# Two pairs of heads one behind the other, with unloads behind the first mask operation and sums over keys in the shares of products

## Chip, core and metric

The kernel runs on one core of one Trainium2 chip. The metric is the device time of one execution in microseconds (us); lower is better. A core has engines that each work through a queue of their own in order and wait for each other by semaphores: TensorE (PE in the profile, its weight loads PEld), VectorE (DVE), ScalarE (ACT), GpSimd (POOL) and SyncE (SP, which issues the transfers here). The products write to PSUM[...].

## The reference

The input x holds 32 batches of 512 rows by 512 features; adj is a 512 x 512 matrix of zeros and ones. Two layers are computed, in float32.

```python
q, k, v = x @ Wq + bq, x @ Wk + bk, x @ Wv + bv          # 8 heads of 64
scores  = einsum(q, k) / 8 + where(adj == 0, -1e9, 0)
x = layernorm(x + einsum(softmax(scores), v))            # layer 0
norm_adj = adj * rsqrt(deg)[:, None] * rsqrt(deg)[None, :]
x = layernorm(x + norm_adj @ (x @ weight) + bias)        # layer 1
```

## The kernel before

All work is one stream over **blocks**. A block is a batch b and a pair of heads g; the eight heads make four pairs, taken in ORDER = (0, 2, 1, 3), so that 32 batches give S = 128 blocks, and `at = k % 4` is the place of block k within its batch. The loop over k writes the program of all engines out by hand: the four compute engines are wrapped in `InOrder`, which pins each instruction to the place where the code issues it. Transfers on SP are not pinned.

**What one turn of the loop does.** `scores(k)` makes the scores of a block in two halves (jj = 0, 1) of two tiles each: per tile TensorE multiplies keys with queries for two heads at once (64 rows each), VectorE takes the minimum with 60 and subtracts the mask (255 where adj is zero), and ScalarE takes the exponential in place. Between the two halves stands `fold` of the block before: VectorE transposes the sums over keys in 32 x 32 blocks and reduces them. Then `values(k - 1)` multiplies the exponentials of the block before with the values (64 columns for each head); the products of a block add up in one PSUM bank, the tile "av" (one buffer). VectorE then unloads that bank by a transpose into "yb" (one buffer), and four transfers on SP put yb into the rows of YT. `accumulate` lets GpSimd add the exponentials over the four tiles of a block; half of that is put off (`pending`, `put_off`) to places in the work that follows, and what is still pending is drained at the top of the next turn.

**The share.** Behind the attention products of each turn, `run(shares.pop(0))` runs a share of all other work: values, keys and queries of the next batch (`values_of`, `keys_and_queries`, each seven pieces of products with a half-size scheme of sums and differences), the normalising of the batch before (`finish`: inverse, scale, add, measure, root, norm, low, lift, judge), and its graph product (`convolve`: first, parts, second, measure, root, store). A list `side` is written out by hand once a batch, at `at == 1`: the pieces of `main` in order, with `beside` giving by number what follows a piece. `cut` splits it by counting pieces with products: eight to a share, four shares to a batch. A piece takes the next PSUM buffer by turns of three buffers of two banks ("wide") and one of one bank ("narrow"); the score tiles take the same three wide buffers.

**Buffers that matter here.** "e" holds exponentials, six buffers, so three halves of blocks; a half's buffers come free when its `values` products and its `accumulate` are done. "acc" has two buffers, freed by `fold`. "kq" has five, "yT" two.

**Lines.** Every instruction passes through the wrapper at line 44, so the profile's lines tell nothing and its rows are told apart by tile names: "sc" are score tiles, "av" the values' sums, "mm" the other products, "e<-sc,maskT" the mask operation, "acc" the sums over keys, "folded" their reduction, "yb<-av" the unload, "parts" sums and differences ahead of the graph product's second half, "lo" and "hi" the two parts of its first factor.

Of the kernel before, what the change touches and what calls it, by code (L numbers as in the profile page):

```python
# [49 lines left out]
def unshifted(  # L50
# [29 lines left out]
    B, N, D = x.shape  # L80
    NT = N // P
    DT = D // P
    G = H // 2
# [315 lines left out]

    E, ACC, AV, SM, YT, HI, LO = {}, {}, {}, {}, {}, {}, {}  # L400

    def scores(s):

        b, g, jj = s
        E[s] = [work.tile([P, 2, N], F32, name="e", bufs=6) for _ in range(2)]
        for l in range(2):
            j = 2 * jj + l
            e = E[s][l]
            p = psum.tile([P, 2, N], F32, name="sc", **WIDE)
            for k in range(2):  # L410
                r = slice(k * HD, (k + 1) * HD)
                tensor.matmul(p[:, k, :], KQ[b, g][r, 0, ts(j, P)], KQ[b, g][r, 1, :], start=True, stop=True)
            vector.scalar_tensor_tensor(
                e, p, CUT, maskT[:, j, None, :].to_broadcast([P, 2, N]), op0=ALU.min, op1=ALU.subtract
            )
            scalar.activation(e, e, AF.Exp)

    def accumulate(s, ls=(0, 1)):

# [14 lines left out]
            for l in ls:  # L434
                gpsimd.tensor_add(ACC[b, g][0], ACC[b, g][0], E[s][l])

    def values(s):

        b, g, jj = s
        e = E.pop(s)  # L440
        if jj == 0:
            AV[b, g] = psum.tile([P, N], F32, name="av")
        av = AV[b, g]
        for l in range(2):
            j = 2 * jj + l
            for k in range(2):
                tensor.matmul(
                    av[k * HD : (k + 1) * HD, :], V[b][:, j, ts(2 * g + k, HD)], e[l][:, k, :],
                    start=j == 0, stop=j == NT - 1,
                )  # L450
        if jj == 0:
            return
        if (b, g) == blocks[-1]:
            turned = work.tile([P, N], F32, name="avT", tag="yb", bufs=1)
            scalar.copy(turned[:, :HALF], av[:, :HALF])
            vector.tensor_copy(turned[:, HALF:], av[:, HALF:])
            AV[b, g] = turned
            return

        yb = work.tile([P, 4, NT, 32], F32, name="yb", bufs=1)
        vector.transpose(
            yb.rearrange("p l i s -> p i l s"), av.rearrange("p (i r l) -> p i l r", i=NT, l=4)
        )
        if g == ORDER[0]:
            if b < B - 1:
                YT[b] = acts.tile([P, NT, D], F32, name="yT")
            else:
                YT[b] = wv[:, :NT].rearrange("p k u o -> p k (u o)")  # L470
        for q in range(4):
            nc.sync.dma_start(
                YT[b][:, :, (4 * g + q) * 32 : (4 * g + q + 1) * 32],
                yb[32 * q : 32 * (q + 1)],
            )
# [326 lines left out]
    def run(pieces):  # L802
        for _, f, args in pieces:
            f(*args)

    def cut(pieces, counts):

        lists = [[]]
        left = list(counts)
        for piece in pieces:  # L810
            if piece[0] > 1:
                if not left[0]:
                    left.pop(0)
                    lists.append([])
                left[0] -= 1
            lists[-1].append(piece)
        return lists
# [6 lines left out]
            accumulate(*pending.pop(0))  # L824

    put_off = [(0, more, ())]

    ORDER = (0, 2, 1, 3)
    blocks = [(b, g) for b in range(B) for g in ORDER]
# [23 lines left out]
    for k in range(S + 1):  # L853
        b, at = divmod(k, G)
        if at == 1:
            if 1 < b < B - 1:
                load_residual(b - 1)
            if b + 2 < B:
                load_x(b + 2, 0)
            if b + 1 < B:  # L860
                main, kq = keys_and_queries(b + 1, 0), keys_and_queries(b + 1, 1)
                if b:
                    main = values_of(b + 1) + main
                turn0, turn1 = turns(b + 2) if b + 2 < B else ([], [])
                main += kq[:5]
            if b == 0:
                w1_parts = [(0, weigh_part, (w1, gpsimd, i)) for i in range(4)]
                exact = [(0, compare, (m,)) for m in range(NT)]
                main += kq[5:]
                beside = {  # L870
                    0: exact[:1], 2: put_off, 3: put_off + exact[1:2], 6: put_off + [(0, degrees, ())],
                    7: w1_parts[:1] + put_off, 8: w1_parts[1:2], 9: w1_parts[2:3], 10: put_off + turn0,
                    11: put_off + w1_parts[3:], 12: exact[2:3],
                }
                inner, rest = turn1, exact[3:]
                side = early[5:6] + put_off + early[6:] + put_off
                side += sum(([piece] + beside.get(i, []) for i, piece in enumerate(main)), [])
                shares = cut(side, (4, 4, 4, 4))
            elif b < B - 1:
                f, c = finish(b - 1), convolve(b - 1)  # L880
                norm, low, grow, measure = f["norm"], f["low"], f["grow"], f["measure"]


                beside = {
                    0: rest[:1] + put_off, 1: put_off + rest[1:3], 2: rest[3:4], 3: rest[4:5] + f["inverse"],
                    4: rest[5:6] + f["scale"][:2], 5: rest[6:7] + f["scale"][2:] + f["add"], 6: rest[7:],
                    8: measure[:2] + put_off, 9: measure[2:] + f["root"] + put_off, 10: norm[:1], 11: norm[1:2],
                    12: norm[2:3] + low[:1], 13: low[1:2], 14: norm[3:] + low[2:3], 16: low[3:] + put_off,
                    17: put_off, 18: f["lift"] + turn0 + f["judge"],
                }  # L890
                side = sum(([piece] + beside.get(i, []) for i, piece in enumerate(main)), [])
                side += c["first"] + c["parts"] + grow + kq[5:] + turn1[:1]
                s = c["second"]
                if b < B - 2:
                    side += put_off + s[:1] + put_off + s[1:3] + turn1[1:2] + s[3:4] + turn1[2:3] + s[4:5]
                    side += turn1[3:4] + s[5:6] + c["measure"][:1] + turn1[4:] + s[6:]
                    rest = c["measure"][1:] + c["root"] + c["store"]
                    shares = cut(side, (8, 8, 8, 8))
                else:
                    held, h, last = c, s, finish(b)  # L900
                    scale, add = last["scale"], last["add"]
                    side += h[:1] + last["inverse"] + h[1:2] + scale[:2] + h[2:3] + scale[2:] + add
                    shares = cut(side, (8, 8, 8, 4))
            else:
                f, c, last = last, convolve(b - 1), finish(b)
                s, first, low, lift, pairs = c["second"], c["first"], f["low"], f["lift"], last["pairs"]
                within = low[:1]
                shares = [
                    h[3:4] + f["measure"] + f["root"] + h[6:] + f["norm"],
                    h[4:5] + low[1:3] + h[5:6] + low[3:] + lift + f["judge"] + put_off + put_off + last["early"] + first[:2]  # L910
                    + held["measure"][:2] + first[2:3] + held["measure"][2:] + first[3:] + c["parts"] + f["grow"],
                    held["root"] + s[:2] + pairs[0] + pairs[1],
                    [],
                ]


        while pending:
            more()
        if k == S - 2:
            load_residual(B - 1)  # L920
        if k < S:
            scores((*blocks[k], 0))
        else:
            turn_of["n"], turn_of["order"] = 0, (WIDE, dict(tag="narrow"), dict(tag="av"))
        if k == 0:
            run(two)
            early = values_of(1)
            run(early[:2])
        elif at == 1 and b:
            run(inner)  # L930
            inner = []
        if k and blocks[k - 1][0] < B - 1:
            fold(*blocks[k - 1])
        if k < S - 3:
            scores((*blocks[k], 1))
            turn_of["n"] = 0
        if k:
            values((*blocks[k - 1], 0))
            if k == S:
                sums(B - 1, 1)  # L940
            values((*blocks[k - 1], 1))
            if k == S - 2:
                sums(blocks[k - 1][0], (k - 1) % G // 2)
                run(within)
# [13 lines left out]
            load_residual(B - 2)  # L958
        if k == 0:
            run(early[2:4] + put_off + put_off + early[4:5])  # L960
        elif shares:
            run(shares.pop(0))

    count = small.tile([P, 1], F32, name="count")
# [306 lines left out]
```

## Time and profile before

| | |
|---|---|
| median of 3 runs | 2784.55 us (2784.54 to 2784.9) |
| profiled execution, its own time | 2784.45 us |
| its span in the profile | 2782.6 us, 34,623 instructions |
| busy: PE, PEld | 2760.6 us (99%), 1878.3 us (68%) |
| busy: DVE, ACT, POOL | 2232.0 us (80%), 1050.6 us (38%), 1795.6 us (65%) |
| granted TensorE clock | 0.999 |
| moved by transfers | 141.06 MB, 51 GB/s on the mean |

Busy time is the union of an engine's instructions over the span. The ends of matmuls are modelled and overlap the starts of the next, so a busy PE says that it never ran dry, not that each step is as short as it can be: steps are read from the starts. Each float32 product stands in the trace as two records, so a block shows 16 records "sc" and 16 "av" for its 8 and 8 products. The profiled execution lies within 0.1 us of the median and 1.85 us above its own span.

### The profile page before, as it was taken

To read this page: it belongs to the slowest core of one execution; us is meant where nothing else is said; L and a number is where in the kernel's file an instruction comes from. 1 tells how busy PE (TensorE), PEld (TensorE's weight loads), DVE (VectorE), ACT (ScalarE), POOL (GpSimd) and SP (SyncE) were. 2 spreads that over 40 slices of the span, in tenths; PEclk is the share of its full clock that TensorE was granted. 3 is DMA by queue.
4 is the path that set the end of the run, shared out by engine and by line. 5 is a ranking of instruction groups with operands and counts; after the bars stand their busy time and mean duration, and the time that the engine had idled before them with its cause. 6 is when DMAs were issued, how large, how long until landed. Compare 5 with 4: busy or idle time off the path is not lost.

```text
span 2782.6 us, 34623 instructions
## 1 busy us (share of the span) xinstructions
PE 2760.6 (99%) x12540; PEld 1878.3 (68%) x12540; DVE 2232.0 (80%) x3199; ACT 1050.6 (38%) x1324; POOL 1795.6 (65%) x1171
## 2 busy tenths in 40 slices
PE   9999999999999999999999999999999999999997
PEld 7666666666666666666666666666666666666665
DVE  5878877788777888777887778877788877788787
ACT  2234333343333433334433334333343433443344
POOL 3666676666666666766667666666666676666756
PEclk9999999999999999999999999999999999999999
DMA  4111122112221111211112211222111121111211
GB/s 122 35 31 45 52 59 57 42 36 53 57 57 43 46 50 50 58 45 42 50 50 61 57 42 35 54 57 57 42 42 54 50 57 46 42 50 50 61 38 51
DMA packets 379109, 141.06 MB, mean 51 GB/s; under 512 B 277808, under 2 KB 345392, under 8 KB 378928
## 3 DMA queue, kind: packets, MB, share of 16 engines
q1 hardware_dynamic: 377776, 137.17, 19.1%
q8 instruction: 101, 1.65, 0.2%
q10 hardware_dynamic: 1152, 1.57, 0.2%
q14 instruction: 80, 0.66, 0.1%
HBM read 71.83 MB, written 33.55 MB: 38 GB/s over the span
## 4 chain that ended last, share of the span: by engine, by line
PE 97%; DVE 2%; POOL 1%; issue 0%; DMA 0%; ACT 0%; POOLq 0%; DVEq 0%
PE mm L44 64%; PE sc L44 17%; PE av L44 16%; DVE st L44 0%; POOL xT L44 0%; POOL acc L44 0%; DVE wv L44 0%; DVE e L44 0%; DMA xr<-in_x_dram 0%; DVE y L44 0%; DVE u L44 0%; DVE mv L44 0%; DVE xT L44 0%; DVE ve L44 0%; DVE low L44 0%
## 5 line engine op out<-in xcount | busy, mean ns | idle before, releaser
L44 ACT ACTIVATE e<-e 128x1024 f32<-128x1024 f32 x512 | 540.7, 1057 | 852.3 <-DVE e L44 758.9
L44 POOL TENSOR_TENSOR acc<-acc,e 128x1024 f32<-128x1024 f32 x248 | 597.2, 2408 | 155.6 <-ACT e L44 148.1
L44 DVE SCALAR_TENSOR_TENSOR e<-sc,maskT 128x1024 f32<-128x1024 f32 x512 | 601.6, 1217 | 59.1 <-PE sc L44 59.0
L44 POOL TENSOR_TENSOR acc<-e 128x1024 f32<-128x1024 f32 x126 | 298.1, 2366 | 368.9 <-ACT e L44 368.9
L44 PE MATMUL sc<-kq 64*128 64x512 f32 x2048 | 476.3, 603 | 0.6 <-DVE v L44 0.3
L44 PE MATMUL mm<-xT,wk 128*128 128x256 f32 x1792 | 469.6, 384 | 0.0
L44 PE MATMUL av<-e,v 128*64 128x512 f32 x2048 | 467.9, 599 | 0.0
L44 PE MATMUL mm<-xT,wq 128*128 128x256 f32 x1792 | 459.9, 379 | 0.0
L44 PEld LDWEIGHTS mm<-xT,wk 128*128 128x128 f32 x1792 | 332.3, 190 | 117.9 <-DVE e L44 74.6
L44 PE MATMUL mm<-wv,xT 128*128 128x256 f32 x1792 | 402.2, 382 | 1.1 <-PE mm L44 0.6
L44 PEld LDWEIGHTS mm<-wv,xT 128*128 128x128 f32 x1792 | 335.9, 190 | 72.0 <-DVE e L44 23.5
L44 PEld LDWEIGHTS mm<-xT,wq 128*128 128x128 f32 x1792 | 340.5, 190 | 46.3
L44 PEld LDWEIGHTS av<-e,v 128*64 128x64 f32 x2048 | 135.4, 136 | 316.3 <-issue 275.4
L44 PEld LDWEIGHTS sc<-kq 64*128 64x128 f32 x2048 | 183.7, 186 | 229.1 <-issue 142.7
L44 POOL TENSOR_TENSOR yT<-yT,xr 128x512 f32<-128x512 f32 x124 | 153.9, 1275 | 132.8 <-DVE yT L44 132.8
L44 PE MATMUL mm<-w,zT 128*128 128x256 f32 x992 | 224.6, 379 | 0.0
L44 DVE TENSOR_TENSOR kq<-u,mm 128x512 f32<-128x512 f32 x128 | 87.8, 686 | 159.7 <-PE mm L44 156.5
L44 PEld LDWEIGHTS mm<-w,zT 128*128 128x128 f32 x992 | 188.2, 190 | 27.0 <-DVE wq L44 0.8
L44 PE MATMUL mm<-adjT,hi 128*128 128x512 f32 x496 | 202.1, 407 | 0.0
L44 PE MATMUL mm<-adjT,lo 128*128 128x512 f32 x496 | 195.4, 394 | 0.0
L44 DVE TENSOR_TENSOR e<-e,mm 128x512 f32<-128x512 f32 x224 | 151.3, 676 | 49.0 <-PE mm L44 48.9
L44 POOL TENSOR_TENSOR xT<-xT 128x512 f32<-128x512 f32 x126 | 159.1, 1274 | 38.9 <-DVE xT L44 32.2
(144 smaller groups left out, 3218.4 us busy)
## 6 DMA issues: line engine op xcount, KB each, us to landing
out_dram<-y SPq DMA_DIRECT2D x127, 256.0 KB, 2.1
x<-in_x_dram SPq DMA_DIRECT2D x248, 128.0 KB, 2.7
yT<-yb SPq DMA_DIRECT2D x496, 64.0 KB, 2.4
xr<-in_x_dram SPq DMA_DIRECT2D x122, 256.0 KB, 3.2
wk<-in_L_gnn_Wk_dram SPq DMA_DIRECT2D x8, 128.0 KB, 4.6
wq<-in_L_gnn_Wq_dram SPq DMA_DIRECT2D x8, 128.0 KB, 4.4
yT<-in_adj_dram SPq DMA_DIRECT2D x1, 1024.0 KB, 6.1
w<-in_L_gnn_weight_dram SPq DMA_DIRECT2D x2, 512.0 KB, 7.7
```

What stands on the lines that cost most here:

```text
L44: return self.tc.keep_in_program_order(op(*args, **kwargs))
```

## The change

For the blocks from 4 to 123 (`double`), two turns of the loop are run one behind the other without a share between them. The even turn (at 0 or 2) runs scores, the sums over keys of the block before, and values; then the odd turn (at 1 or 3) runs its scores and values; then follows one share of sixteen pieces instead of eight. In the even turn the unload of "av" is left out; it is issued in the odd turn, behind the first of its four mask operations. The sums over keys (`fold`) of the even block, which would stand between the halves of the odd turn, are kept in a list and run at a place in the share. The list `beside` is shifted by about one piece from number 2 on, and the put-off additions, `lift` and the last `low` are moved. No operation on data is added or left out.

```diff
-    def scores(s):
+    def scores(s, between=()):
...
             scalar.activation(e, e, AF.Exp)
+            run(between)
+            between = ()
...
-        if jj == 0:
-            return
+        if jj and not later:
+            unload_values(b, g)
+
+    def unload_values(b, g):
+        av = AV[b, g]
...
+    folds = []
+    def fold_first():
+        if folds:
+            fold(*folds.pop(0))
...
-                shares = cut(side, (4, 4, 4, 4))
+                shares = cut(side, (4, 4, 8))
...
                 beside = {
-                    0: rest[:1] + put_off, 1: put_off + rest[1:3], 2: rest[3:4], 3: rest[4:5] + f["inverse"],
-                    4: rest[5:6] + f["scale"][:2], 5: rest[6:7] + f["scale"][2:] + f["add"], 6: rest[7:],
-                    8: measure[:2] + put_off, 9: measure[2:] + f["root"] + put_off, 10: norm[:1], 11: norm[1:2],
-                    12: norm[2:3] + low[:1], 13: low[1:2], 14: norm[3:] + low[2:3], 16: low[3:] + put_off,
-                    17: put_off, 18: f["lift"] + turn0 + f["judge"],
+                    0: rest[:1] + put_off, 1: folded + put_off, 2: rest[1:2], 3: rest[2:4], 4: rest[4:5] + f["inverse"],
+                    5: rest[5:6] + f["scale"][:2], 6: rest[6:7] + f["scale"][2:] + f["add"], 7: rest[7:],
+                    9: measure[:2], 10: measure[2:] + f["root"], 11: norm[:1], 12: norm[1:2] + low[:1],
+                    13: low[1:2], 14: norm[2:3], 16: norm[3:] + low[2:3],
+                    17: low[3:] + f["lift"] + put_off + put_off + folded, 18: turn0 + f["judge"],
                 }
...
-                    shares = cut(side, (8, 8, 8, 8))
+                    shares = cut(side, (16, 16))
...
-                    shares = cut(side, (8, 8, 8, 4))
+                    shares = cut(side, (16, 8, 4))
...
+        double = G <= k < S - G
...
-            scores((*blocks[k], 0))
+            scores((*blocks[k], 0), [(0, unload_values, blocks[k - 2])] if double and at % 2 else ())
...
-        elif at == 1 and b:
+        elif k == G:
             run(inner)
-            inner = []
-        if k and blocks[k - 1][0] < B - 1:
+        if k and not (double and at % 2) and blocks[k - 1][0] < B - 1:
             fold(*blocks[k - 1])
...
+        if double and at % 2:
+            folds.append(blocks[k - 1])
...
-            values((*blocks[k - 1], 1))
+            values((*blocks[k - 1], 1), double and at % 2 == 0)
...
-        elif shares:
+        elif shares and (at % 2 or not double):
             run(shares.pop(0))
```

More of the change, by code (lines that the diff above doesn't have):

```diff
@@ L435, in accumulate, with values @@
                 gpsimd.tensor_add(ACC[b, g][0], ACC[b, g][0], E[s][l])
-    def values(s):
+    def values(s, later=False):
         b, g, jj = s
@@ L877, in unshifted @@
                 side += sum(([piece] + beside.get(i, []) for i, piece in enumerate(main)), [])
-                shares = cut(side, (4, 4, 4, 4))
+                shares = cut(side, (4, 4, 8))
             elif b < B - 1:
-                f, c = finish(b - 1), convolve(b - 1)
+                f, c, folded = finish(b - 1), convolve(b - 1), [(0, fold_first, ())]
                 norm, low, grow, measure = f["norm"], f["low"], f["grow"], f["measure"]
                 beside = {
-                    0: rest[:1] + put_off, 1: put_off + rest[1:3], 2: rest[3:4], 3: rest[4:5] + f["inverse"],
-                    4: rest[5:6] + f["scale"][:2], 5: rest[6:7] + f["scale"][2:] + f["add"], 6: rest[7:],
-                    8: measure[:2] + put_off, 9: measure[2:] + f["root"] + put_off, 10: norm[:1], 11: norm[1:2],
-                    12: norm[2:3] + low[:1], 13: low[1:2], 14: norm[3:] + low[2:3], 16: low[3:] + put_off,
-                    17: put_off, 18: f["lift"] + turn0 + f["judge"],
+                    0: rest[:1] + put_off, 1: folded + put_off, 2: rest[1:2], 3: rest[2:4], 4: rest[4:5] + f["inverse"],
[3 more added lines that the diff above has]
+                    17: low[3:] + f["lift"] + put_off + put_off + folded, 18: turn0 + f["judge"],
                 }
```

## The prediction

> **What bounds the kernel now.** I read the page first: the shares of busy time, then the chain that ended last.
>
> ```profile
> PE 2760.6 (99%) x12540; PEld 1878.3 (68%) x12540; DVE 2232.0 (80%) x3199; ACT 1050.6 (38%) x1324; POOL 1795.6 (65%) x1171
> ...
> PE 97%; DVE 2%; POOL 1%; issue 0%; DMA 0%; ACT 0%; POOLq 0%; DVEq 0%
> ```
>
> TensorE never runs dry, so only its own steps can get shorter. A stretch of the chain gives them (start, length, what):
>
> ```profile
> 1000.92 3.63 PE sc L44 x16
> 1004.55 3.58 PE av L44 x16
> 1008.13 14.01 PE mm L44 x64
> 1022.15 3.63 PE sc L44 x16
> ```
>
> A block is 3.63 + 3.58 us of attention and 14.01 us of share. The timeline of TensorE's starts gives the plain step inside a share:
>
> ```profile
> 1009.03 1.03 PE L44 MATMUL mm<-xT,wq 128*128 128x256 f32 x4
> ...
> 1021.12 1.03 PE L44 MATMUL mm<-xT,wq 128*128 128x256 f32 x4
> 1022.08 1.13 PE L44 MATMUL sc<-kq 64*128 64x512 f32 x4
> ```
>
> 56 records in 12.09 us: 0.2159 each, so 64 would take 13.81, and the share takes 14.01. **Entering and leaving a share costs 0.20 us** beyond its products. Is a change from values straight to scores dearer? Near the end the kernel has it already:
>
> ```profile
> 2721.35 3.65 PE L44 MATMUL av<-e,v 128*64 128x512 f32 x16
> 2724.93 1.99 PE L44 MATMUL sc<-kq 64*128 64x512 f32 x8
> 2726.85 1.35 PE L44 MATMUL mm<-w,zT 128*128 128x256 f32 x5
> ```
>
> Sixteen value records last 3.58 with scores behind them, as with a share behind them (first stretch), and eight score records last 1.92, as elsewhere there. So leaving out one share boundary saves 0.20 us and costs nothing.
>
> **What the skill says.** "TensorEngine Tiling (Array Packing)", Key Properties: "Changing tiling mode (not just tile) drains the TensorE". Scores use 64 rows, values 64 columns, shares the whole array: three modes. The trace agrees: the first step into each is about 0.1 us longer. "TensorE: Matmul & The Clock Gate", Step-by-step: in a stream the drain of one product overlaps the fill of the next; 0.2159 us for records of 0.379 us agrees. "SBUF — State Buffer", SBUF: two separate sides: a VectorE operation with two SBUF inputs and a GpSimd one that reads SBUF exclude each other. "lo" with 0.726 at least, 0.753 median, 1.361 at most fits that; moved rows need both values.
>
> **The change, part by part.** *Boundaries.* Blocks 4 to 123 make 60 pairs; each loses one share boundary: 60 x 0.20 = **-11.8 us** (0.197 unrounded). Nothing is added to TensorE. All else costs nothing only if TensorE never waits, so I laid the queues out with the durations shown, time 0 being the first score record of a pair. TensorE: scores to 3.63, values 7.21, scores 10.84, values 14.42, then sixteen pieces of 8 x 0.216 = 1.73 us.
>
> *Mask operations, unloads and half the folds.* VectorE's order in a single block now is
>
> ```profile
> 1023.25 2.36 DVE L44 SCALAR_TENSOR_TENSOR e<-sc,maskT 128x1024 f32<-128x1024 f32 x2 [0.31 <-PE sc L44]
> 1025.53 1.24 DVE L44 STREAM_TRANSPOSE acc<-acc 128x1024 f32<-128x1024 f32 x1
> 1026.80 1.22 DVE L44 TENSOR_REDUCE folded<-acc 128x32 f32<-128x1024 f32 x1
> 1027.93 2.35 DVE L44 SCALAR_TENSOR_TENSOR e<-sc,maskT 128x1024 f32<-128x1024 f32 x2
> 1030.19 0.71 DVE L44 STREAM_TRANSPOSE yb<-av 128x512 f32<-128x512 f32 x1
> ```
>
> with scores starting at 1022.08: first mask at 1.17, fourth done at 8.2. In a pair the fifth tile is ready at 7.21 + 1.17 = 8.4, masked by 9.6. The eighth score tile takes the fifth's wide buffer at 7.21 + 0.53 + 5 x 0.43 = 9.9: 0.3 to spare. The unload behind the fifth mask runs 9.6 to 10.3; the second values need the bank at 10.84: 0.5 to spare. Had both folds (2.4 each) stayed, both margins would be gone.
>
> *Exponential buffers.* With six, the seventh mask needs the first half of the even block released: by its values (first tile read by 10.84 + 0.47 + 0.59 = 11.9) and by GpSimd's addition (from 4.7 for 2.4, so 7.1). Seventh and eighth masks end at 13.1 and 14.3. The share's second and third pieces (16.2, 18.0) take those score buffers: hidden with 3 us. The second unload waits for the transfers out of yb: issued over 2.65 from 10.3, each landing in 2.4 (page), so about 15; done by 15.7, before the share's first result at 16.6. SP's queue ahead of them holds loads of x only, whose buffers are free by time 0.
>
> *First share.* GpSimd: addition to 15.4, two put off to 20.2. VectorE: first pieces from 16.6; moved fold 19.0 to 21.3; then without pause piece sums (0.6), statistics (0.8), inverse (1.25), four scales (2.4) to 30.9. It lags by 3 us at most; a product buffer is asked for again 5.2 us after its result. Until now a 7.2 us block of attention stood between scale and statistics and gave GpSimd time for its four additions (4.98). Now: additions 30.9 to 36.0, last statistics 37.1, root on GpSimd (1.02 + 0.20) 38.8, norm and hi on ScalarE (0.8 + 0.7 each) 40.2 and 41.7, second lo done 42.4, last sum for keys 43.4 (its product is ready at 42.7). The next pair's first mask can start at 43.65. VectorE is on time, **with about half a microsecond** to spare on the chain of lo.
>
> *Second share.* Last lo done at 20.0, read by TensorE's graph product at 19.7 + 7 x 0.234 = 21.3. Behind it on GpSimd: lift (5.1) and two additions (4.8), so the second "parts" (1.25 each) is done at 32.4; TensorE needs it after three pieces, four graph products (1.87) and four pieces: 34.1. Spare 1.3 and 1.7.
>
> *Start and end.* The first batch's shares (4, 4, 8) and the last (16, 8, 4) do the same work; the moved transpose of x (1.24) stands once in the first pair: under 1 us. Bound of this, both ways: 1 us.
>
> Sum: 2784.45 (profiled execution) - 11.8 = 2772.65; the median stands 0.1 above: **2772.7**.
>
> **Rivals.** (1) *No wait*, above: 2771.5 to 2774. (2) *Small waits*: a margin of 0.3 to 0.5 is missed by a few tenths in one of the two places, 30 or 60 times: 0.1 to 0.2 us x 30 to 60 = 2 to 6 us back: 2774 to 2779. For it: the layout has errors of that size. Against it: in the run before all clusters of one place repeat to within 0.01 us at the median, and after numbers 8 to 15 the first mask is on time in every batch. (3) *Slower: the statistics chain in the first share.* If the chain scale, additions, statistics, root, hi, lo ends late, so does the next pair's first mask, and the fourth score tile, which takes the first's buffer, waits. Before number 0 of `beside` that mask is now 0.13 late and the wait is 0.008 us, so lateness L costs L - 0.12, 30 times. It eats the gain at L = 0.12 + 11.8/30 = 0.51, and the kernel is slower by over 0.2% from L = 0.12 + (11.8 + 5.6)/30 = 0.70; since the chain has half a microsecond of slack and I may misjudge it by one or more, L = 1.2 gives +32 - 12: 2805. Against it: I counted 0.5 to spare. (4) *Saving eaten*: waits of about 0.2 us a pair, or a boundary price that appears elsewhere (the two straight changes at the end are all that show it): 2779 to 2790.
>
> **How the numbers follow.** Chances: (1) 0.58, (2) 0.16, (4) 0.13, (3) 0.13. A measurement of this kernel can tell about 0.2%, 5.6 us, from no change; (1) and (2) lie beyond it: faster 0.74, same 0.13, slower 0.13. The range takes in (1), (2) and nearly half of (4): 2771.5 to 2784; the likeliest case alone is 2771.5 to 2774.
>
> **What would show it.** Right: 60 shares of 128 records at 27.8 us where two of 64 took 28.0; value runs 3.58 us before scores; DVE's first mask 1.18 behind the first score in nearly all pairs. Wrong: score records more than 0.43 apart inside a run, waits of "sc" for "e" on DVE or "parts" on POOL, "av" waiting for "yb". If score runs stay at 3.63 and the time is above 2779, my boundary price was wrong; if they lengthen, a margin was.

## The result and the profile after

The changed kernel takes 2773.06 us (median of 6 runs, 2772.62 to 2774.16) where the kernel before takes 2784.93 on the same chip (2784.54 to 2785.46): ratio 0.9957, 95% interval 0.9946 to 0.9967. The forecast was 2772.7. The profiled execution took 2773.32 us, its span 2771.4.

The page of after, busy time first:

```profile
PE 2748.6 (99%) x12540; PEld 1882.6 (68%) x12540; DVE 2237.2 (81%) x3199; ACT 1053.9 (38%) x1324; POOL 1786.7 (64%) x1171
...
ACT 0%; issue 0%
```

The same 12,540 records of products take 12.0 us less of TensorE's time; the other engines run as many instructions as before. The second line is the chain that ended last. On this trace it was followed back no further than one activation of ScalarE and says nothing. The starts on TensorE's timeline say it instead (start, length, what; one pair and the first share behind it):

```profile
968.14 3.71 PE L44 MATMUL sc<-kq 64*128 64x512 f32 x16
971.78 3.65 PE L44 MATMUL av<-e,v 128*64 128x512 f32 x16
975.36 3.70 PE L44 MATMUL sc<-kq 64*128 64x512 f32 x16
979.00 3.65 PE L44 MATMUL av<-e,v 128*64 128x512 f32 x16
982.58 8.90 PE L44 MATMUL mm<-wv,xT 128*128 128x256 f32 x40
...
1010.63 1.56 PE L44 MATMUL sc<-kq 64*128 64x512 f32 x6
```

Scores 3.64, values 3.58, scores 3.64, values 3.58: no run is longer than in a single block. The share lasts 1010.63 - 982.58 = 28.05, of which 0.22 are two small products of "inverse" that stood in this share of 14.23 before (from the chain of the kernel before):

```profile
1072.38 14.23 PE mm L44 x66
```

14.01 + 14.23 - 28.05 = 0.19 saved.

VectorE in the next pair, whose first score starts at 1010.63:

```profile
1011.80 2.36 DVE L44 SCALAR_TENSOR_TENSOR e<-sc,maskT 128x1024 f32<-128x1024 f32 x2 [0.31 <-PE sc L44]
1014.08 1.24 DVE L44 STREAM_TRANSPOSE acc<-acc 128x1024 f32<-128x1024 f32 x1
1015.35 1.22 DVE L44 TENSOR_REDUCE folded<-acc 128x32 f32<-128x1024 f32 x1
1016.48 2.35 DVE L44 SCALAR_TENSOR_TENSOR e<-sc,maskT 128x1024 f32<-128x1024 f32 x2
1019.02 1.23 DVE L44 SCALAR_TENSOR_TENSOR e<-sc,maskT 128x1024 f32<-128x1024 f32 x1 [0.20 <-PE sc L44]
1020.16 0.71 DVE L44 STREAM_TRANSPOSE yb<-av 128x512 f32<-128x512 f32 x1
1020.79 1.19 DVE L44 SCALAR_TENSOR_TENSOR e<-sc,maskT 128x1024 f32<-128x1024 f32 x1
1022.68 2.36 DVE L44 SCALAR_TENSOR_TENSOR e<-sc,maskT 128x1024 f32<-128x1024 f32 x2 [0.70 <-PE av L44]
1025.40 0.72 DVE L44 STREAM_TRANSPOSE yb<-av 128x512 f32<-128x512 f32 x1 [0.36 <-DMA yT<-yb]
```

The fifth mask starts at 8.39 and waits 0.20 for its scores, so VectorE was early. The unload ends at 10.24. The seventh mask waits for the values to release its exponential buffer, the second unload for the transfers out of yb. Over the span these two waits, new in this kernel, are (waits on VectorE: total us, times, longest):

```profile
DVE e L44 <- PE av L44: 42.1, 60, 1.1
DVE yb L44 <- DMA yT<-yb: 36.1, 60, 1.5
```

Sixty each, one a pair, 78 us of waiting on VectorE. TensorE's own waits of "sc" for "e" add up to 0.4 us over the span.

A steady measure is used from here: the time **per batch**, from the first score record of block 8 to that of block 56, over twelve batches. Before: 85.70 us. After: 85.31. That is 0.39 for two boundaries. It leaves out the start and the last 110 us. The kernels with pairs differ there by up to 1 us before the first score and by up to 1.5 us in the last stretch, also where their instructions there are the same.

### The profile page after: what moved, and what is told of

Same layout as the page of the kernel before. It is cut to its first block, busy times and chain, and to the rows that moved or that the text cites. A ratio compares the mean times of both kernels' runs of the same rounds, so it can differ in the third digit from the quotient of the medians.

```text
span 2771.4 us, 34559 instructions
## 1 busy us (share of the span) xinstructions
PE 2748.6 (99%) x12540; PEld 1882.6 (68%) x12540; DVE 2237.2 (81%) x3199; ACT 1053.9 (38%) x1324; POOL 1786.7 (64%) x1171
## 3 DMA queue, kind: packets, MB, share of 16 engines
q10 hardware_dynamic: 1152, 1.57, 0.2%
## 5 line engine op out<-in xcount | busy, mean ns | idle before, releaser
L44 POOL TENSOR_TENSOR acc<-acc,e 128x1024 f32<-128x1024 f32 x248 | 589.1, 2375 | 89.7 <-ACT e L44 77.5
L44 PE MATMUL mm<-xT,wk 128*128 128x256 f32 x1792 | 463.3, 381 | 0.0
L44 POOL TENSOR_TENSOR yT<-yT,b_r 128x512 f32<-128x512 f32 x124 | 157.3, 1304 | 140.2 <-DVE lo L44 140.2
L44 ACT ACTIVATE y<-y,add,rstd 128x512 f32<-128x512 f32 x127 | 96.2, 805 | 317.3 <-POOL add L44 317.3
```

Source lines behind the costliest of these rows:

```text
L44: return self.tc.keep_in_program_order(op(*args, **kwargs))
```

## The experiments

**Does the gain go by boundaries?** Three kernels. First, the moved list alone, with no two turns behind each other:

```diff
-        double = G <= k < S - G
+        double = False
-                    shares = cut(side, (16, 16))
+                    shares = cut(side, (8, 8, 8, 8))
```

(with the other two cuts and the place of `inner` as before.)

> The moved list of work beside the products is kept, but no two turns are run one behind the other: four shares of eight pieces again, unloads and sums over keys at their old places. Theory (the gain is the share boundaries): no boundary is saved, so the time of before, 2784.5 within 1 us. Rival (the gain comes from the new order of the work beside): about 2773.

It took 2813.39 us (ratio to before 1.0099, 1.0082 to 1.0116), 86.55 per batch. Neither theory had this: the list by itself loses 0.84 us a batch. Around the fourth block of a batch, first score at 1031.61, the timeline of all engines has

```profile
1027.57 5.12 POOL L44 TENSOR_TENSOR acc<-acc,e 128x1024 f32<-128x1024 f32 x2
...
1029.25 1.22 DVE L44 SCALAR_TENSOR_TENSOR lo<-yT,dis,hi 128x512 fp32r<-128x512 f32 x1 [1.16 <-ACT hi L44]
1030.39 0.68 DVE L44 TENSOR_TENSOR kq<-e,mm 128x512 f32<-128x512 f32 x1
1030.99 2.25 DVE L44 SCALAR_TENSOR_TENSOR lo<-yT,dis,hi 128x512 fp32r<-128x512 f32 x1
...
1033.76 2.34 DVE L44 SCALAR_TENSOR_TENSOR e<-sc,maskT 128x1024 f32<-128x1024 f32 x2
...
1035.03 1.13 PE L44 MATMUL sc<-kq 64*128 64x512 f32 x4 [0.57 <-DVE e L44]
```

Two "lo" operations read two SBUF inputs each and take 1.22 and 2.25 us where 0.75 is usual, while GpSimd's put-off additions run: in single blocks the moved list leaves those to the drain behind root. The first mask is 0.97 late (1033.76, against 1031.61 + 1.18), and TensorE's fourth score tile waits. In a pair the same list meets no addition at that place, and all 124 "lo" of after take 0.72 to 0.75. This is my rival of the late statistics chain, in a kernel where it is real, and at its price: 0.97 less the 0.12 that the prediction allows is 0.85. The Trainium skill's "SBUF — State Buffer" (section SBUF: two separate sides) names exclusion between two-input VectorE operations and GpSimd ones that read SBUF. The trace agrees: in list_only the 60 "lo" that overlap with GpSimd take 1.22 to 2.26 us and the 64 others 0.72 to 0.75, and the second one above ends 0.55 behind the end of GpSimd's additions (1033.24, against 1032.69).

So the second kernel, half of the blocks in pairs, was not a clean one:

```diff
+        double = G <= k < S // 2
+                    shares = cut(side, (16, 16) if k < S // 2 else (8, 8, 8, 8))
```

> Blocks 4 to 63 in pairs, blocks 64 to 127 as before: 30 share boundaries saved instead of 60. Theory: 30 x 0.197 = 5.9 us off before, about 2778.8, and 98 changes from products of a share to scores in the trace instead of 68. Rival (one gain at the start or the end, or a gain that does not go by boundaries): 2773 or 2784.

2793.18 us: its single half carries the loss of the moved list (a stop of 0.74 us at the fourth score tile of fifteen batches). The third keeps the list of before for the single half:

```diff
+                if k < S // 2:
+                    beside = {...}      # moved list
+                else:
+                    beside = {...}      # list of before
```

> Blocks 4 to 63 in pairs with the moved list, blocks 64 to 127 with shares of eight and the list of before: the amount of pairing alone is halved, which the first such kernel did not do cleanly. Theory: 85.31 us for each paired batch and 85.70 for each other, 30 boundaries saved, 5.9 us off before. Rival (pairing gains only as a whole): no gain or all of it.

2780.41 us (ratio 0.9982, 0.9975 to 0.9988). Its batches take 85.31 in the paired half and 85.70 in the single one, each to 0.01 the number of the whole kernel of that kind. Its trace has 99 changes from a share to scores, where before has 130 and after 70. The gain goes by boundaries. The total is 4.96 below the median of before beside it, not 5.9; its runs spread over 2779.3 to 2782.3. Part of the rest is seen in its trace: the first score comes 0.37 later than in before's, the first block with the old list (65) stops for 0.32, and the last stretch, from the first score of block 124, is 0.63 longer.

**What holds the margins in a pair?** The sum over keys left where it was, between the halves of the odd block:

```diff
-        if k and not (double and at % 2) and blocks[k - 1][0] < B - 1:
+        if k and blocks[k - 1][0] < B - 1:
-        if double and at % 2:
-            folds.append(blocks[k - 1])
```

> Pairs, with the sums over keys of the even block left between the halves of the odd block instead of in the share. My prediction said that both margins in the pair would go. Laid out again: fifth mask and unload stand ahead of that sum, so they stay in time; but the sum needs GpSimd's additions of the even block, done at about 13.0 us from the pair's first score, so VectorE waits from 11.4 to 13.0, seventh and eighth masks end at 16.6 and 17.8 instead of 13.1 and 14.3, and the second piece of the share, which takes the seventh tile's buffer at 16.25, waits about 0.4 us. Theory: 60 x 0.4 to 0.5 = 24 to 30 us on top of 2773: 2797 to 2803. Rival (VectorE has a fifth of its time idle, so the place of the sum does not matter): 2773.

2822.48 us (1.0133, 1.0117 to 1.0150). The place is the one expected, the size larger. VectorE, GpSimd and TensorE in a pair that starts at 1074.56:

```profile
1084.73 1.18 DVE L44 SCALAR_TENSOR_TENSOR e<-sc,maskT 128x1024 f32<-128x1024 f32 x1
1087.83 1.25 DVE L44 STREAM_TRANSPOSE acc<-acc 128x1024 f32<-128x1024 f32 x1 [1.91 <-POOL acc L44]
1089.11 1.22 DVE L44 TENSOR_REDUCE folded<-acc 128x32 f32<-128x1024 f32 x1
1090.24 2.34 DVE L44 SCALAR_TENSOR_TENSOR e<-sc,maskT 128x1024 f32<-128x1024 f32 x2
```

```profile
1082.98 4.81 POOL L44 TENSOR_TENSOR acc<-acc,e 128x1024 f32<-128x1024 f32 x2 [1.23 <-ACT e L44]
```

```profile
1089.00 1.99 PE L44 MATMUL mm<-wv,xT 128*128 128x256 f32 x8
1091.51 4.80 PE L44 MATMUL mm<-wv,xT 128*128 128x256 f32 x21 [0.52 <-DVE e L44]
```

GpSimd's additions end 13.2 after the pair's start; VectorE waits 1.91 for them with two masks queued behind. The share's second piece, due at 1089.00 + 0.10 + 1.73 = 1090.83, starts at 1091.51: 0.68; the other pair of a batch stops for 0.57. The step after each stop is longer by 0.10. I had laid out 0.4 to 0.5 in all. Per batch 86.77, or 0.73 a pair.

Is it the 2.4 us of the sum, or the wait? The same sum, behind the fourth mask of the odd block:

```diff
         if double and at % 2:
-            folds.append(blocks[k - 1])
+            fold(*blocks[k - 1])
```

> Pairs, with the sums over keys of the even block on VectorE behind the fourth mask of the odd block: still in the pair, so VectorE does as much there as with the sums left between the halves, but later than GpSimd's additions end and behind all masks. Theory (the wait for GpSimd ahead of two masks was the cost, not the 2.4 us): no wait of TensorE, 2773 within 1.5 us. Rival (VectorE has no room for a second sum in a pair, so it must move to the share): near the 2822 of the kernel with the sums between the halves.

2773.78 us (0.9960, 0.9944 to 0.9975), 85.31 per batch, as the change. VectorE at the end of a pair:

```profile
1022.73 2.36 DVE L44 SCALAR_TENSOR_TENSOR e<-sc,maskT 128x1024 f32<-128x1024 f32 x2 [0.70 <-PE av L44]
1025.00 1.23 DVE L44 STREAM_TRANSPOSE acc<-acc 128x1024 f32<-128x1024 f32 x1
1026.27 1.22 DVE L44 TENSOR_REDUCE folded<-acc 128x32 f32<-128x1024 f32 x1
1027.41 0.71 DVE L44 STREAM_TRANSPOSE yb<-av 128x512 f32<-128x512 f32 x1
```

No wait ahead of the sum, none behind it. It is the place in VectorE's queue that costs, ahead of two masks and ahead of GpSimd's end; the share is one of two good places. The run moves the sum behind both at once, so it does not part the wait from the 2.4 us. An estimate from the folds_stay lines does: the seventh mask ends there at about 1091.4, which delays TensorE by 0.78. Without the 1.91 of waiting, or without the 2.4 of the sum, it would end over 1 us before the share needs its buffer. The two together make the loss.

The unload at its old place, behind the fourth mask:

```diff
-            scores((*blocks[k], 0), [(0, unload_values, blocks[k - 2])] if double and at % 2 else ())
+            scores((*blocks[k], 0))
-            values((*blocks[k - 1], 1), double and at % 2 == 0)
+            values((*blocks[k - 1], 1))
```

> Pairs, with the unload of the even turn at its old place, behind the fourth mask and ahead of the fifth. Theory: unload from 8.2 to 8.9 us, fifth mask ends at about 10.1 instead of 9.6, and the eighth score tile, which takes its buffer at 9.9, waits 0.2 to 0.3 us in each of 60 pairs: 12 to 18 us, 2785 to 2791, the gain gone. Rival (the unload hides behind 80% busy VectorE wherever it stands): 2773.

2788.81 us (1.0013, 1.0006 to 1.0020): within the expectation, and the gain is gone. The unload now stands ahead of the fifth mask (VectorE), and the run of scores grows from 3.63 to 1070.76 - 1066.82 = 3.94 (TensorE):

```profile
1067.83 0.71 DVE L44 STREAM_TRANSPOSE yb<-av 128x512 f32<-128x512 f32 x1
1068.46 2.32 DVE L44 SCALAR_TENSOR_TENSOR e<-sc,maskT 128x1024 f32<-128x1024 f32 x2
```

```profile
1066.82 4.02 PE L44 MATMUL sc<-kq 64*128 64x512 f32 x16
1070.76 3.65 PE L44 MATMUL av<-e,v 128*64 128x512 f32 x16
```

Per batch 85.81: 0.25 a pair on the mean (0.31 in the pair shown, 0.19 in the other of a batch). Moving one 0.7 us operation behind one mask is worth 15 us here.

Both at their old places (the two edits together):

> Pairs alone: the sums over keys of the even block stay between the halves of the odd block and the unload of the even turn stays at its old place. Theory: the two waits do not add, because TensorE's lateness of 0.25 us at the eighth score tile gives the late masks that much time: 2797 to 2805, near the kernel where only the sums stay. Rival (independent costs): the sum of both single losses on top of 2773.

2822.26 us, 86.75 per batch, no worse than with the sums alone. As expected the waits do not add: in the trace the eighth score tile waits 0.15 plus 0.10 on the mean of both pairs, and the share's second piece 0.37 plus 0.10 instead of 0.63 plus 0.10. The size was missed as above. With both operations at their old places the pairs thus lose 36 us on before, where the whole change brings 12. These kernels have the moved list; pairs with the list of before were not run.

**How much is to spare on the statistics chain?** One or two needless operations at its end:

```diff
-                    13: low[1:2], 14: norm[2:3], ...
+                    13: low[1:2] + low[1:2], 14: norm[2:3], ...      # late_2: three times
```

> One more VectorE operation of 0.67 us in the first share of each batch, the second lo computed twice (same result), at the tightest place of the statistics chain. The trace of after shows 0.33 and 0.31 us idle on VectorE ahead of the last sum for keys and ahead of the next pair's first mask, and the first mask may be 0.12 late: 0.76 to spare. Theory: hidden, 2773 within 1 us. Rival (no slack, every us on that chain counts): 0.67 x 30 = 20 us, 2793.

2774.08 us (0.9959, 0.9945 to 0.9974), 85.31 per batch: hidden.

> Two more VectorE operations of 0.67 us at that place (the second lo computed three times). Theory: 1.34 - 0.76 = 0.58 us of wait for 30 pairs, 17 us: 2788 to 2792. Rival (slack larger than measured, VectorE far from deciding): 2773.

2793.65 us (1.0027, 1.0016 to 1.0039), 85.94 per batch, 0.63 more in each. VectorE and TensorE, with the pair starting at 1017.38:

```profile
1016.47 2.32 DVE L44 SCALAR_TENSOR_TENSOR lo<-yT,dis,hi 128x512 fp32r<-128x512 f32 x3
1018.71 0.68 DVE L44 TENSOR_TENSOR kq<-e,mm 128x512 f32<-128x512 f32 x1
1019.31 1.22 DVE L44 SCALAR_TENSOR_TENSOR e<-sc,maskT 128x1024 f32<-128x1024 f32 x1
```

```profile
1020.58 1.13 PE L44 MATMUL sc<-kq 64*128 64x512 f32 x4 [0.35 <-DVE e L44]
```

The first mask is 0.75 late (1019.31, against 1017.38 + 1.18). The fourth score tile stops for 0.53 and its next step is 0.10 longer: 0.63. I had 0.58, from two errors that nearly cancel. Three "lo" take 2.32 where one takes 0.75, so the two needless ones add 1.57 and not 1.34; and 1.57 - 0.63 = 0.94 was to spare, not 0.76. In late_1, with one, the first mask starts at its usual 1.18.

**More of the same: four blocks.** If only boundaries count, four blocks one behind the other save one more a batch.

```diff
-                    shares = cut(side, (16, 16))
+                    shares = cut(side, (32,))
...
-            scores((*blocks[k], 0), [(0, unload_values, blocks[k - 2])] if double and at % 2 else ())
+            scores((*blocks[k], 0), [(0, unload_values, blocks[k - 2])] if double and at else ())
...
+        elif double and at == 3:
+            fold(*blocks[k - 3])
...
-        if double and at % 2:
-            folds.append(blocks[k - 1])
+        if double and at == 3:
+            folds += [blocks[k - 1], blocks[k], blocks[k - 2]]
...
-            values((*blocks[k - 1], 1), double and at % 2 == 0)
+            values((*blocks[k - 1], 1), double and at < 3)
...
-        elif shares and (at % 2 or not double):
+        elif shares and (at == 3 or not double):
```

> Four blocks one behind the other and one share of 32 pieces for batches 1 to 30. To have sums over keys for four blocks, the third block's take one buffer that two small ones of the half-size scheme (idle there) now share; one sum over keys stands in the fourth block, three in the share. Theory: 30 more boundaries saved, 5.9 us off after, 2767, if no wait comes in; VectorE has 1.3 to 1.9 us of idle time per block in such a run, so it keeps up. Rival (the run of attention is now long enough for VectorE or GpSimd to fall behind: GpSimd needs 7.15 us of additions per block where TensorE needs 7.21): score tiles wait, above 2773.

2768.64 us (0.9937, 0.9920 to 0.9954). TensorE in a batch:

```profile
1062.61 3.65 PE L44 MATMUL av<-e,v 128*64 128x512 f32 x16
1066.19 3.70 PE L44 MATMUL sc<-kq 64*128 64x512 f32 x16
1069.83 3.65 PE L44 MATMUL av<-e,v 128*64 128x512 f32 x16
1073.41 3.70 PE L44 MATMUL sc<-kq 64*128 64x512 f32 x16
```

Values 3.58 and scores 3.64, as in pairs; in the steady part only block 38 is held up, by 0.30. Per batch 85.11 in all other batches of that part: 0.20 below after, as one boundary should be (85.13 over the twelve batches with that stop). The whole is 4.4 below after's median instead of 5.9; its first score comes 0.6 later than in after's trace, and its last stretch, from the first score of block 124, takes 111.9 us instead of 110.9. I suspected a load that I had moved:

```diff
+        if k == S - G - 1:
+            load_residual(B - 2)          # ahead of the share again
         if k == 0:
             run(early[2:4] + put_off + put_off + early[4:5])
         elif shares and (at == 3 or not double):
             run(shares.pop(0))
-        if k == S - G - 1:
-            load_residual(B - 2)
```

> Four blocks one behind the other as in quad, with the load of the residual of the last batch but one issued ahead of the share, its place in after, and not behind it. Per batch 0.195 us below after as in quad: 5.6 to 5.9 us for 30 batches. Theory: that load's place made quad 1.0 us later in its last 30 us, so 2767.5. Rival (that loss is something else): quad's 2768.6 again.

2769.04 us (0.9941, 0.9928 to 0.9955), and a last stretch of 112.4: the load's place is not the cause. The loss falls on products "sc<-adjT" some 60 us behind block 125's first score, with VectorE, ScalarE and GpSimd within 0.02 us of after's times up to that place. The windows of the profile name it. Quad first, then the same place in after (the last three numbers are granted TensorE clock, DMA share, GB/s):

```profile
2731.00:2735.00 4.00, 3.85 (x10) 3.07 (x11) 2.96 (x6) 2.76 (x4) 0.85 (x2) 0.57 0.02 4
2736.00:2740.00 4.00, 3.37 (x13) 2.47 (x14) 2.95 (x6) 2.77 (x4) 1.33 (x2) 1.00 0.00 2
```

In quad the mean of 0.57 over 4 us is half the clock for 3.4 us, and the "sc<-adjT" steps of 0.23 become 0.42; quad_2 shows the same (0.57). It is no matter of four blocks: folds_stay and unload_first, whose instructions from block 124 on are those of after in the same order, have it too (0.58 in unload_first; 112.0 and 112.3 us), while after, after_again, fold_last, late_1, late_2 and both_stay do not (110.8 to 111.2). The later start and this stretch together are about the 1.5 us that quad lacked. Why the clock drops there in some traces is not shown.

> The changed kernel itself, unedited, on the chip of quad_2 for a comparison side by side: 2773 within 1 us.

2773.85 us (2773.56 to 2774.03) beside quad_2's 2768.53 to 2769.62: four blocks are 4.8 us faster than the change on one chip, and no run of one reaches the other's. Four blocks are the fastest version tried.

## Why the prediction was right

**The boundary.** Read as 0.197 us from three stretches of the trace before, 60 times. Measured 0.39 for two per batch in after and in half of half_old_list, and 0.20 for the third in quad. Right in mechanism and size. The steps show what is saved: any change of the kind of product makes the last step before it about 0.10 longer, and the first step behind it too (0.05 for values, where the prediction said about 0.1 for each kind). Values to a share to scores are two changes, values to scores one. What happens inside TensorE at a change, these runs do not show. Nor do records of 0.379 us that start every 0.216 show an overlap by themselves, since their ends are modelled. The sign "60 shares of 128 records at 27.8 us" was off in form: in the steady part a batch has one share of 130 records at 28.05 and one of 128 at 28.38, the latter with longer graph products, each 0.19 below its two halves before (14.01 + 14.23 and 14.01 + 14.56).

**Changing straight from values to scores costs nothing extra.** Right: 3.58 us for the values in every pair, though only two such changes were there to read it from.

**The layout of a pair.** Laid out against seen, from the pair's first score: fifth mask 8.4 and 8.39, unload done 10.3 and 10.24, seventh mask 11.9 and 12.05, eighth done 14.3 and 14.41, second unload done 15.7 and 15.49, last sum for keys in the first share done 43.4 and 43.36 (from 968.14 to 1011.50). In the second share the last lo was laid out to be done at 20.0 and is at 19.73, the second "parts" at 32.4 and 32.28, needed by TensorE at 34.1 and 34.10. Two waits that I named are there, hidden.

**Margins.** The 0.3 us ahead of the eighth score tile was 0.12 in truth. In unload_first the fifth mask ends 2.83 and 2.71 behind its block's first score, where 2.40 is usual, and costs 0.31 and 0.19: 0.12 of each delay is free. My sum took the buffer at the start of the eighth tile's record; the mask has to end about 0.16 before that. The fifth mask came at 8.39 where I had 8.4, so the margin held, but an error like that at the seventh mask (0.15) would have used it up: here the forecast had some luck, and rival (2) was nearer than I counted. The half microsecond on the chain of lo was 0.94 (late_2): on the safe side.

**What was wrong.** "Had both folds (2.4 each) stayed, both margins would be gone" named the wrong reason. The sum in the odd turn stands behind the fifth mask and the unload and touches neither margin. It costs 0.73 a pair because it waits for GpSimd and stands ahead of two masks whose buffers the share takes (folds_stay, fold_last). And the margin of 3 us that I gave these buffers holds only with the sum out of the way.

**The sum.** Forecast for the profiled execution 2772.65, measured 2773.32. Of the 0.67, the last stretch from block 124's first score gives 0.44 (110.49 before, 110.93 after). The first pairs give 0.27: in after blocks 5 and 6 are held up by 0.72 and 0.43, where before has 0.88 at block 6. Both lie inside the bound of 1 us for start and end. The moved list was taken as free; in pairs no wait comes of it, in single blocks it costs 28 us (list_only). I had not priced it without pairs, and the forecast did not need it.

## What to carry to other kernels

When one engine is busy throughout, measure what its changes between kinds of work cost from the starts of its instructions, and count the changes: grouping like work can pay without removing an instruction. Then lay out the other engines' queues over one group, from durations of the trace, and look for the operation that stands ahead of one which a buffer waits for: here 0.7 us in the wrong place of VectorE's queue cost 15 us, and 2.4 us in the right place nothing. An order of work tuned for one grouping should be priced again under another. And where a loss finds no cause in the program, look at the granted clock of that stretch first.

## What the runs showed of the hardware beyond what I expected

A stop of TensorE inside a run shows in two steps. In late_2, folds_stay, both_stay and unload_first the step after each stop is longer by 0.10 us: 0.53 where 0.42 is usual for a pair of score records, 0.32 where 0.216 is usual in a share. Those are the lengths of the first steps after a change of the kind of product, so the gap between two starts tells 0.10 us less than such a stop costs.

The whole loss is no more than the lateness. The fourth score tile of a block takes the buffer of the block's first. When the mask on that first tile ends 2.52 us behind the block's first score record, the run of scores is longer by 0.01 (every other pair of after); at 2.71 and 2.83 by 0.19 and 0.31 (unload_first), at 3.15 by 0.63 (late_2), at 3.36 by 0.84 (list_only). So in these runs each microsecond past 2.52 costs one microsecond, with nothing on top: rival (3) of the prediction, lateness less 0.12, had the right price.
